# A fourth set of expert weights, and the ranked experts' first load moved behind a gather

## Chip, cores and metric

The kernel runs on one core of a Trainium2 chip. The metric is device time in microseconds (us), the median of three runs. The host only pads x to 3328 rows, pads and transposes the adjacency matrix, and cuts the padding off the result.

## What is computed

One layer of a graph network with 3327 tokens of 256 features, then a mixture of 16 experts of which every token uses two:

```python
# graph attention: x = x + LN(softmax-weighted mean over neighbours of h), h = layernorm(x) @ W, 4 heads of 64
x = x + gnn(layernorm(x), adj, W, a, gamma, beta)
# experts, on xn = layernorm(x)
logits = xn @ gate_w + gate_b                 # (3327, 16)
top_probs, top_idx = top_k(softmax(logits), 2)
dispatch = one_hot(top_idx) * top_probs / sum(top_probs)
hidden = silu(xn @ w1[e]) * (xn @ w2[e])      # w1, w2: 16 x 256 x 512
x = x + sum_e dispatch[:, e] * (hidden @ w3[e])   # w3: 16 x 512 x 256
```

All products are in float32. One expert's three matrices are 0.5 MB each, 1.5 MB together.

## The kernel before

**Two phases.** The graph phase works on 26 tiles of 128 rows in 7 groups. TensorE (PE) multiplies each 0/1 adjacency tile with the rows of h, which are split into a high and a low part (lines 584 and 585), and the matrix streams in on the queue of SyncE (SP). After a group's sums, `finish` normalises the rows, stores them to the DRAM tensor `normed` together with their two experts and weights, and adds the row numbers to per-expert lists. The expert phase walks 19 lists of rows. Lists 0 to 2 are the rows of experts 0 to 2 among the first five groups; they start while the last two groups are being finished. Lists 3 to 5 are the rows of the same three experts from the last two groups (at most 128 rows each). These are what the change's title calls the last groups' first lists. Lists 6 to 18 are the other 13 experts, ranked by how many rows they have, with room for 512 rows down to 336.

**One list** (`take_list`). GpSimd (POOL) gathers the rows of `normed` by an indirect DMA for each 128 rows (line 956) into one of three buffers `xe`; VectorE (DVE) picks each row's weight out of what was gathered (`weigh`, lines 962 and 964, the work `wd`); PE turns the rows (line 1027, result copied by ScalarE, ACT, line 1034); PE multiplies with w1 and w2 in four pieces (line 971), ACT applies silu (line 1044), DVE multiplies (`hid`, line 1047); PE multiplies with w3 (lines 978 and 982); DVE or ACT scales (`y`); POOL adds the rows to the output by an indirect DMA (line 985).

**Weights.** Expert 0's weights go to borrowed buffers. All others are loaded by SP with three DMAs (lines 326 to 328) into a ring of sets of three tiles, `("w", i)`. There are 3 sets: experts 1 and 2 take two of them early and keep them until lists 4 and 5 are done; list 6's expert takes the third. In what follows "w6" is the load for list 6, "w7" the one for list 7, and so on. Which expert list 6 has is known on the chip only: `all_lists` ranks the experts (`names`, line 893 on), and DVE copies the expert numbers into the integer table `table[:, 0]` (line 896), from which SP reads a register (`value_load`, line 1161) before the three DMAs.

**Who sets the order.** Each engine's instructions are written in an order that a planner works out at build time. Every piece of work has an engine, an assumed cost, a rank, works it comes after, and buffers it uses; 80 greedy orders with small random offsets on the works of `finish` are tried, and the one with the shortest replay is written. The works named in `after` only shape this order. On the chip an instruction waits for what its data need: SP's `value_load` waits for the DVE copy into `table`, and a weight DMA waits for the last reader of the set it overwrites. `load_more` (line 941) reads a flag into a register on all engines; a loop for lists that outgrow their room stands at the end and is not entered here.

Of the kernel before, what the change touches and what calls it, by code (L numbers as in the profile page):

```python
# [78 lines left out]
EARLY = 3  # L79
# [135 lines left out]
def gnn_moe(ctx: ExitStack, tc: tile.TileContext, x, adj_t, W, a, gamma, beta, gate_w, gate_b, w1, w2, w3, out):  # L215
    nc = tc.nc
# [64 lines left out]
    expert = const.tile([P, NL], F32, name="expert")  # L281
# [3 lines left out]
    table = const.tile([P, 2, NL], I32, name="table")  # L285
# [54 lines left out]
    gnn, ffn = ExitStack(), ExitStack()  # L340
# [5 lines left out]
    PE, DVE, ACT, POOL, SP = "PE", "DVE", "ACT", "POOL", "SP"  # L346
    T, POOLS = {}, {}
# [18 lines left out]
    def few_h(key):  # L366
# [1 line left out]
                "rs": tiny.tile([P, 2, GT], F32, name="rs", bufs=SLOTS["few_h"])}  # L368

    SLOTS = {"pa": 4, "pt": 2, "ph": 2, "stage": 3, "mask": 3, "pay": 2, "xt": 2, "xnt": 2, "agg": 2, "hp": 2, "hc": 2,  # L370
             "few": 3, "few_h": 3, "xe": 3, "hid": 2, "gate": 3, "y": 6, "w": 3, "weight": 4}
    MAKE = {
        "pa": lambda key: ps_agg.tile([P, CAP], F32, name="pa"),
        "pt": lambda key: ps_tr.tile([P, CAP], F32, name="pt"),
# [23 lines left out]
    plan = Plan(SLOTS, take)  # L398

    def once(key, make):  # L400

        if key not in T:
            T[key] = make()
        return T[key]

    def psum(key):
        return T[key]
# [429 lines left out]
    def numbers(dst, lists, name):  # L837

        empty = tiny.tile(list(lists.shape), F32, name=name, bufs=1)
        nc.vector.tensor_scalar(empty, lists, 0.0, NONE, op0=ALU.is_equal, op1=ALU.mult)  # L840
        nc.vector.scalar_tensor_tensor(dst, lists, -1.0, empty, op0=ALU.add, op1=ALU.add)
# [26 lines left out]
    def all_lists(counted, lists):  # L868
        key = ("ph", "all")

        def make(name, shape):
            return once(("all", name), lambda: tiny.tile([P] + shape, F32, name=name, bufs=1))

        def across(ap):
            return ap[:, None, :].to_broadcast([P, NR, NR])

        def along(ap):
            return ap[:, :, None].to_broadcast([P, NR, NR])

        def ranks():  # L880

            pl = psum(key)
            tokens_of = make("tokens_of", [NE])
            key_, rank, by = make("key", [NR]), make("rank", [NR]), make("by", [NR, NR])
            nc.vector.tensor_copy(tokens_of, pl[:, :NE])
            nc.vector.scalar_tensor_tensor(key_, tokens_of[:, EARLY:], float(NE), number[:, EARLY:], op0=ALU.mult,
                                           op1=ALU.subtract)
            nc.vector.tensor_tensor(by, across(key_), along(key_), op=ALU.is_gt)
            nc.vector.tensor_reduce(rank, by, AX.X, ALU.add)

        def names():
            rank, hotr, by = make("rank", [NR]), make("hotr", [NR, NR]), make("by", [NR, NR])
            nc.vector.tensor_tensor(hotr, across(rank), along(number[:, :NR]), op=ALU.is_equal)
            nc.vector.tensor_tensor(by, hotr, across(number[:, EARLY:]), op=ALU.mult)
            nc.vector.tensor_reduce(expert[:, 2 * EARLY:], by, AX.X, ALU.add)
            nc.vector.tensor_copy(table[:, 0], expert)

        def order():
            return T["hp", "all"].rearrange("p t d -> p (t d)")[:, :NR * CT * NR].rearrange("p (r t e) -> p r t e", r=NR, t=CT)

        def numbered():
            numbers(make("numbered", [NR, CT]), listed[:, EARLY:NE, :], "empty2")

        def sorted_():
            nc.vector.tensor_tensor(order(), make("numbered", [NR, CT]).rearrange("p e t -> p t e")[:, None, :, :].to_broadcast(
                [P, NR, CT, NR]), make("hotr", [NR, NR])[:, :, None, :].to_broadcast([P, NR, CT, NR]), op=ALU.mult)

        def by_ranks():
            nc.vector.tensor_reduce(make("by_rank", [NR, CT]), order(), AX.X, ALU.add)

        def ranked():
            by_rank = make("by_rank", [NR, CT])
            nc.vector.tensor_copy(index[2], by_rank)
            in_out(out_index[2], by_rank, "behind2")

        def rest():

            hotr, by, tokens_of = make("hotr", [NR, NR]), make("by", [NR, NR]), make("tokens_of", [NE])
            full, some = make("full", [NL]), make("some", [1])
            nc.vector.tensor_copy(count[:, EARLY:2 * EARLY], tokens_of[:, :EARLY])  # L920
            nc.vector.tensor_tensor(by, hotr, across(tokens_of[:, EARLY:]), op=ALU.mult)
            nc.vector.tensor_reduce(count[:, 2 * EARLY:], by, AX.X, ALU.add)
            nc.vector.tensor_scalar(behind[:, 2 * EARLY:], expert[:, 2 * EARLY:], float(LIST), None, op0=ALU.mult)
            nc.vector.tensor_scalar(end, behind, float(LIST), None, op0=ALU.add)
            nc.vector.tensor_add(behind, behind, room)
            nc.vector.tensor_tensor(full, count, room, op=ALU.is_gt)
            nc.vector.tensor_copy(table[:, 1], full)
            nc.vector.tensor_reduce(some, full, AX.X, ALU.max)
            nc.vector.tensor_copy(more, some)

        i = plan.add(DVE, 0.7, (1,), [lists], lambda: indices(1))
        w = plan.add(PE, 0.15, (0,), [counted], lambda: tokens_so_far(key), [key])

        r = plan.add(DVE, 1.1, (3, NG, 0), [w], ranks, [key])
        r = plan.add(DVE, 1.2, (3, NG, 0), [r], names)
        o = plan.add(DVE, 0.55, (3, NG, 1), [lists], numbered)
        for cost, piece_ in ((1.4, sorted_), (0.9, by_ranks), (0.6, ranked)):
            o = plan.add(DVE, cost, (3, NG, 1), [r, o], piece_, [("hp", "all")])

        def load_more():  # L940
            many["value"] = nc.values_load(more[0:1, 0:1], min_val=0, max_val=1)

        plan.add(SP, 0.5, (5,), [plan.add(DVE, 2.2, (4,), [o], rest)], load_more)
        return i, r, o
# [52 lines left out]
    GOT = {}  # L997

    def take_list(i, indexed, stored, weights, opened, order):
# [21 lines left out]
            weigh(T["weight", i], XE[i % 3], len(tiles), expert[:, i:i + 1])  # L1021

        wd = plan.add(DVE, 0.4, (2, i, 9), got, weighed, [xek, ("weight", i)])

        def turned(k):
            for t, _ in tiles:
# [4 lines left out]
        for k in range(KC):  # L1031
            key = ("pt", "list", i, k)
            w = plan.add(PE, 0.13 * len(tiles), rank + (0,), got, lambda k=k: turned(k), [key, xek])
# [18 lines left out]
        for t, mm in tiles:  # L1052
            key, yk = ("ph", "list", i, t), ("y", i, t)
            w = plan.add(PE, 8 * 0.217 / PARTS[mm] + 0.1 * (PARTS[mm] > 1), rank + (9 + t,), hids, lambda t=t, mm=mm, key=key: down_products(
                psum(key), w_of(2), hid(), t, mm), [key, hk] + ([wk] if weights else []))
# [4 lines left out]
            def scale(t=t, mm=mm, key=key, yk=yk, helped=helped):  # L1060
# [9 lines left out]
            w = plan.add(ACT if helped else DVE, 0.48 * PARTS[mm], (2, i), [w, wd], scale, [key, yk, ("weight", i)])  # L1070
            ends.append(plan.add(POOL, 1.87, (1, i), [w] + order, lambda t=t, mm=mm, yk=yk: add_rows(
                T[yk], index_of(i, out_index), t, mm, others, i < EARLY), [yk], landing=2.5))
        return ends

# [18 lines left out]
    for made, c0, c1, c in ((landed, H, H + D, 1.0), (summed, 0, H, 0.5)):  # L1095
        means, subtract = center(w_sb, ("ph", "w", c0), c0, c1)
        w = plan.add(PE, c, (0,), [made], means, [("ph", "w", c0)])
# [11 lines left out]
    w = plan.add(PE, 0.8, (2,), [rest], means, [("ph", "gw")])  # L1109
# [7 lines left out]
    for g in range(NG):  # L1117
# [7 lines left out]
        if g == EARLY_GROUP:  # L1125
            i, c = early_lists(c, l)
            tables = [c]
            ready.update({k: (i, list(stored)) for k in range(EARLY)})
        if g == NG - 1:
            i, ranked, o = all_lists(c, l)  # L1130
# [3 lines left out]

    def switch_pools():
        gnn.close()
        POOLS["wmore"] = ffn.enter_context(tc.tile_pool(name="wmore", bufs=3))
        POOLS["hidden"] = ffn.enter_context(tc.tile_pool(name="hidden", bufs=2))
        POOLS["gates"] = ffn.enter_context(tc.tile_pool(name="gates", bufs=3))

# [6 lines left out]
    def more_weights(key, source):  # L1147
        WE[key] = T["w", key]
        load_weights(WE[key], source())

    opened = plan.add(PE, 0.0, (9,), every, switch_pools)
# [3 lines left out]
    def late_weights(i):  # L1155

        if i < EARLY:
            return plan.add(SP, 1.2, (1, 990 + i), [opened] + GOT[i - 1], lambda: more_weights(i, lambda: i), [("w", i)],
                            landing=2.0, size=size)
        return plan.add(SP, 1.6, (1, 1000 + i), [opened, ranked] + GOT[i - 1], lambda: more_weights(  # L1160
            i, lambda: nc.sync.value_load(table[0:1, 0, i:i + 1], min_val=EARLY, max_val=NE - 1)), [("w", i)],
            landing=2.0, size=size)

    order = []
    for i in range(NL):
        of = i if i >= 2 * EARLY else i % EARLY
        if of not in weights:
# [2 lines left out]
        order = take_list(i, indexed, rows + spare[i if i < 2 else 5 if i == 2 else 0], of, [opened, weights[of]], order)  # L1170
# [4 lines left out]
    with tc.If(many["value"] > 0):  # L1175
        with tc.For_i(0, NL) as i:
            e = nc.values_load(table[0:1, 0, bass.ds(i, 1)], min_val=0, max_val=NE - 1)
            full = nc.values_load(table[0:1, 1, bass.ds(i, 1)], min_val=0, max_val=1)
            w = weight_tiles()
            load_weights(w, e)  # L1180
            with tc.For_i(0, full * (NT // AGAIN)) as c:
# [4 lines left out]
                weight = small.tile([P, AGAIN], F32, name="weight_again")  # L1186
# [12 lines left out]
                hid = POOLS["hidden"].tile([P, JC, CAP], F32, name="hid")  # L1199
# [9 lines left out]
                y = POOLS["gates"].tile([P, CAP], F32, name="s").rearrange("p (t d) -> p t d", d=D)  # L1209
# [37 lines left out]
```

## Time and profile before

| | |
|---|---|
| median of 3 runs | 532.24 us (531.89 to 532.77) |
| the profiled execution | 532.32 us, its span 530.6 us, clock 0.997 |
| PE busy | 517.0 us of the span (97%) |
| DVE, ACT, POOL busy | 274.1, 160.8, 213.3 us |
| weight loads on SP's queue | 15 x 3 DMAs of 512 KB, and expert 0's |
| gathers (L956) and row additions (L985) | 61 each, 1051 ns and 1538 ns on POOL |

Times in the views are microseconds from the start of the span. A line of the timeline gives start, length, engine, source line, operation, output and inputs, shape and how many instructions are merged; in square brackets stands the engine's idle time before it and what ended it. PEld is the loading of weights into PE's array. q0 is the DMA queue of the gathers and row additions, q1 that of SP's DMAs. In the waits view the columns are total us, times, and the longest.

### The profile page before, as it was taken

What the parts mean: (1) busy time and instruction counts of PE and PEld (TensorE: products, weight loads), DVE (VectorE), ACT (ScalarE), POOL (GpSimd) and SP (SyncE); (2) the same over time, 40 slices, a digit from 0 to 9 for tenths busy, and PEclk for the clock granted to TensorE, in tenths of its full rate; (3) what the DMA queues carried; (4) which work ended last, traced back from release to release, by engine and by line L of the source; (5) the groups of instructions that cost most, each with busy time, mean ns of one, the idle gap of its engine ahead of it and who ended that gap; (6) DMA issues with size and microseconds to landing.
All of it is one profiled execution on the core that took longest, in us unless ns stands there. A gap on an engine that the chain in (4) does not pass through costs nothing. (4 is left out here: it accounts for less than half of the span.)

```text
span 530.6 us, 8626 instructions
## 1 busy us (share of the span) xinstructions
PE 517.0 (97%) x3005; PEld 406.5 (77%) x3006; DVE 274.1 (52%) x848; ACT 160.8 (30%) x464; POOL 213.3 (40%) x240
## 2 busy tenths in 40 slices
PE   8999999999999999999898999999999999999995
PEld 5889999999999999777686557566566656666674
DVE  6968554967779799689721222212233233323221
ACT  3461145545362650564222201111111111112110
POOL 4320031311030413566677364373475446522333
PEclk9999999999999999999999999999999999999998
DMA  8934879897879893754648564463465546543222
GB/s 277 361 118 126 287 245 316 257 315 258 255 227 369 261 370 118 220 151 105 182 76 274 136 126 120 96 160 112 101 157 143 141 99 156 141 117 70 30 29 28
DMA packets 63394, 94.63 MB, mean 178 GB/s; under 512 B 4846, under 2 KB 36850, under 8 KB 63348
## 3 DMA queue, kind: packets, MB, share of 16 engines
q1 hardware_dynamic: 52308, 80.04, 46.3%
q0 software_dynamic: 10768, 13.75, 15.3%
q8 instruction: 24, 0.39, 0.3%
q10 hardware_dynamic: 272, 0.26, 0.2%
q14 instruction: 22, 0.18, 0.1%
HBM read 81.55 MB, written 13.90 MB: 180 GB/s over the span
## 5 line engine op out<-in xcount | busy, mean ns | idle before, releaser
L584 PE MATMUL pa<-hi,mk 128*128 128x258 f32 x676 | 167.6, 289 | 1.0 <-DVE mk L561 1.0
L585 PE MATMUL pa<-lo,mk 128*128 128x256 f32 x676 | 163.3, 281 | 0.0
L584 PEld LDWEIGHTS pa<-hi,mk 128*128 128x128 f32 x676 | 127.8, 189 | 2.3 <-DVE mk L561 1.2
L585 PEld LDWEIGHTS pa<-lo,mk 128*128 128x128 f32 x676 | 127.5, 189 | 0.1
L985 POOL DMA_INDIRECT out<-y,out_index x61 | 93.8, 1538 | 59.0 <-DVE y L1065 39.9
L971 PE MATMUL pa<-xt,w1e 128*128 128x400 f32 (+8 forms) x272 | 98.9, 486 | 1.7 <-issue 1.7
L1047 DVE TENSOR_TENSOR hid<-s,pa 128x400 f32<-128x400 f32 (+9 forms) x76 | 40.2, 529 | 116.1 <-PE pa L971 91.8
L956 POOL DMA_INDIRECT x<-normed,index x61 | 64.1, 1051 | 86.5 <-PE pt L1027 64.7
L971 PE MATMUL pa<-xt,w2e 128*128 128x400 f32 (+8 forms) x272 | 98.2, 484 | 0.3
L1044 ACT ACTIVATE s<-pa 128x400 f32<-128x400 f32 (+9 forms) x76 | 35.8, 471 | 199.8 <-PE pa L971 191.5
L982 PE MATMUL ph<-w3e,hid 128*128 128x256 f32 (+2 forms) x400 | 89.5, 380 | 0.0
L982 PEld LDWEIGHTS ph<-w3e,hid 128*128 128x128 f32 (+2 forms) x400 | 73.7, 188 | 10.5 <-issue 0.2
L971 PEld LDWEIGHTS pa<-xt,w2e 128*128 128x128 f32 x272 | 49.5, 190 | 37.6 <-issue 18.7
L971 PEld LDWEIGHTS pa<-xt,w1e 128*128 128x128 f32 x272 | 49.2, 190 | 37.8 <-issue 21.9
L561 DVE TENSOR_SCALAR mk<-sg 128x2048 fp32r<-128x2048 f32 (+2 forms) x49 | 54.2, 1106 | 29.9 <-PE pa L585 28.4
L1065 DVE TENSOR_SCALAR y<-ph,weight 128x256 f32<-128x256 f32 (+5 forms) x54 | 26.0, 482 | 72.2 <-PE ph L982 41.0
L650 POOL TENSOR_TENSOR hp<-csum,c 128x512 f32<-128x512 f32 (+1 forms) x14 | 15.1, 1096 | 65.0 <-DVE c L646 65.0
L478 PE MATMUL ph<-w_sb,xnt 128*128 128x260 f32 x104 | 27.2, 397 | 0.4 <-DVE lo L484 0.3
L1034 ACT COPY xt<-pt 128x512 f32<-128x512 f32 (+2 forms) x38 | 17.4, 505 | 20.1 <-PE pt L1027 18.7
L478 PEld LDWEIGHTS ph<-w_sb,xnt 128*128 128x128 f32 x104 | 17.8, 189 | 4.8 <-issue 1.2
L421 POOL TENSOR_SCALAR rs_x<-spread_x 128x4 f32<-128x4 f32 (+1 forms) x7 | 1.8, 259 | 47.3 <-ACT pay L427 44.1
L1027 PEld LDWEIGHTS pt<-ident,x 128*128 128x128 f32 x122 | 14.3, 141 | 7.1 <-issue 6.1
(181 smaller groups left out, 471.4 us busy)
## 6 DMA issues: line engine op xcount, KB each, us to landing
sg<-in_adj_t SPq DMA_DIRECT2D x25, 1024.0 KB
sg<-in_adj_t SPq DMA_DIRECT2D x20, 768.0 KB
w1e<-in_ffn_w SPq DMA_DIRECT2D x15, 512.0 KB
w2e<-in_ffn_w SPq DMA_DIRECT2D x15, 512.0 KB
w3e<-in_ffn_w SPq DMA_DIRECT2D x15, 512.0 KB
normed<-pay SPq DMA_DIRECT2D x5, 520.0 KB
out<-x SPq DMA_DIRECT2D x5, 512.0 KB
sg<-in_adj_t SPq DMA_DIRECT2D x4, 576.0 KB
```

Source lines behind the costliest of these rows:

```text
L478: nc.tensor.matmul(ph[:, :H + D], T["xnt", g, t][:, k, :], w_sb[:, k, :], start=(k == 0), stop=(k == KC - 1))
L561: nc.vector.tensor_scalar(T[mk][:, :m, :n * P], T[sk][:, :m, :n * P], 0.0, None, op0=ALU.is_gt)
L584: nc.tensor.matmul(pa[:, :D + 2], lhs, HI[mg][:, i, H:], start=first, stop=False)
L585: nc.tensor.matmul(pa[:, :D], lhs, LO[mg][:, i, H:], start=False, stop=left[g, t] == 0)
L956: nc.gpsimd.indirect_dma_start(out=xe[:, t, :], out_offset=None, in_=normed[:limit], in_offset=at_rows(idx, t), bounds_check=limit - 1, oo ...
L971: nc.tensor.matmul(p[:, :n], wt[:, k, j * P:(j + 1) * P], xt[:, k, :n], start=(k == 0), stop=(k == KC - 1))
L982: nc.tensor.matmul(py[:m, :D], hid[:, j, t * P:t * P + m], w3e[:, j, :], start=(j == 0), stop=(j == JC - 1))
L985: i = nc.gpsimd.indirect_dma_start(out=out, out_offset=at_rows(idx, t, m), in_=y[:m], in_offset=None, bounds_check=NP - 1, oob_is_err=Fals ...
L1034: xts.append(plan.add(ACT, 0.1 + 0.9e-3 * m, (1, i), [w], lambda k=k, key=key: nc.scalar.copy(xt()[:, k, :m], psum(key)[:, :m]), [key, xtk]))
L1044: nc.scalar.activation(T["gate", i, j][:, :n], psum(key)[:, :n], AF.Silu)
L1047: nc.vector.tensor_mul(hid()[:, j, :n], T["gate", i, j][:, :n], psum(key)[:, :n])
L1065: nc.vector.tensor_scalar(T[yk][:mm], psum(key)[:mm, :D], weight, None, op0=ALU.mult)
```

## The change

The ring of weight sets has 4 sets instead of 3. The copy of the expert numbers into `table` leaves `names` and becomes a DVE work of its own, `tell`, that is planned after the weights of list 4's rows have been picked (`wd` of list 4, which waits for list 4's gather). The ranked experts' loads come after `tell` instead of after `ranked` (the ranking). In the plan w6 no longer comes after list 5's gather, and the load for a later list comes after the gather two lists before it instead of the one before it.

```diff
     SLOTS = {...
-             "few": 3, "few_h": 3, "xe": 3, "hid": 2, "gate": 3, "y": 6, "w": 3, "weight": 4}
+             "few": 3, "few_h": 3, "xe": 3, "hid": 2, "gate": 3, "y": 6, "w": 4, "weight": 4}
...
             nc.vector.tensor_reduce(expert[:, 2 * EARLY:], by, AX.X, ALU.add)
-            nc.vector.tensor_copy(table[:, 0], expert)
...
         wd = plan.add(DVE, 0.4, (2, i, 9), got, weighed, [xek, ("weight", i)])
+        if i == 2 * EARLY - 2:
+
+            told.append(plan.add(DVE, 0.2, (2, i, 9), [wd, ranked], tell))
...
+    def tell():
+        nc.vector.tensor_copy(table[:, 0], expert)
...
-        POOLS["wmore"] = ffn.enter_context(tc.tile_pool(name="wmore", bufs=3))
+        POOLS["wmore"] = ffn.enter_context(tc.tile_pool(name="wmore", bufs=4))
...
-        return plan.add(SP, 1.6, (1, 1000 + i), [opened, ranked] + GOT[i - 1], lambda: more_weights(
+        return plan.add(SP, 1.6, (1, 1000 + i), [opened] + told + (GOT[i - 2] if i > 2 * EARLY else []), lambda: more_weights(
             i, lambda: nc.sync.value_load(table[0:1, 0, i:i + 1], min_val=EARLY, max_val=NE - 1)), [("w", i)],
             landing=2.0, size=size)
...
-    order = []
+    order, told = [], []
```

`EARLY` is 3, so `2 * EARLY - 2` is list 4 and `i > 2 * EARLY` means list 7 on.

## Prediction

> **What bounds the kernel now.** I read the page first: PE is busy 517.0 of 530.6 us, so at most 13.6 us can be won without making PE's work smaller, and the change removes no PE instruction. The waits of PE come next, because they say whether a weight load or a gather ever stops it.
>
> ```profile
> engine line waited for: us in total, times, longest us
> PE pt L1027 <- DMA x<-normed,index: 2.0, 1, 2.0
> PE pa L971 <- issue: 1.7, 2, 1.0
> ...
> PE pa L584 <- DVE mk L561: 1.0, 1, 1.0
> PE pt L708 <- DVE x L692: 1.0, 2, 0.6
> ```
>
> No line says that PE waited for a weight set. Its longest wait is for a gather: 2.0 us, once. Then the windows, cut where PE's work changes, show where the idle time lies.
>
> ```profile
> 0.00:215.81 215.81, 213.00 (x1718) 201.65 (x1720) 161.61 (x524) 92.60 (x302) 51.34 (x110) 1.00 0.78 257
> 215.81:260.32 44.51, 43.52 (x234) 31.28 (x233) 37.73 (x154) 22.11 (x64) 27.29 (x27) 1.00 0.62 175
> 260.32:262.83 2.51, 0.51 (x4) 0.31 (x3) 1.23 (x7) 0.43 (x2) 1.55 (x2) 1.00 0.61 205
> 262.83:288.10 25.27, 23.32 (x160) 20.59 (x160) 6.46 (x23) 6.67 (x21) 19.49 (x17) 1.00 0.59 145
> 288.10:524.71 236.61, 236.61 (x895) 152.70 (x893) 66.61 (x141) 39.01 (x75) 111.35 (x86) 1.00 0.48 114
> ```
>
> First number after the stretch: its length; second: PE busy. From 288.10 (list 6's first product, the first ranked expert) to PE's end PE never idles, so the time is set by when PE gets there. Idle before that: 2.81 us in the graph phase, 0.99 before 260.32, 2.00 at the gather, 1.95 after it. The 1.95 us are no DMA's: they stand at 280.9 to 285.0, and PE's semaphore there rises every 0.73 to 0.77 us per group of four 128-column matmuls that the records space by 0.45 us, so the recorded starts run ahead of PE, and the gap is PE's own arrears. Third, the timelines of PE, POOL and SP around the wait.
>
> ```profile
> 260.32 0.38 PE L1027 MATMUL pt<-ident,x 128*128 128x128 f32 x2
> 262.70 0.30 PE L1027 MATMUL pt<-ident,x 128*128 128x128 f32 x1 [2.00 <-DMA x<-normed,index]
> 262.83 1.06 PE L971 MATMUL pa<-xt,x 128*128 128x128 f32 x8
> ```
>
> ```profile
> 254.42 1.09 POOL L956 DMA_INDIRECT x<-normed,index  x1 [0.98 <-DVE behind L846]
> 255.81 1.82 POOL L956 DMA_INDIRECT x<-normed,index  x1 [0.31 <-issue]
> 257.94 1.00 POOL L956 DMA_INDIRECT x<-normed,index  x1 [0.30 <-issue]
> ```
>
> ```profile
> 254.81 0.40 SPq L326 DMA_DIRECT2D w1e<-in_ffn_w  x1
> 255.39 0.39 SPq L327 DMA_DIRECT2D w2e<-in_ffn_w  x1
> 256.48 0.00 SPq L328 DMA_DIRECT2D w3e<-in_ffn_w  x1
> 277.72 0.38 SPq L326 DMA_DIRECT2D w1e<-in_ffn_w  x1
> ```
>
> The three POOL lines are the gathers of lists 3, 4 and 5. w6 is issued at 254.81, before two of them, although the plan puts it after list 5's: on the chip it waits only for the copy into `table`, done at 253.60, and its set is free. Its packets on q1 run from 255.86 to 261.81. List 4's gather, issued at 255.81, lands at 262.56 (the last event on its semaphore), 6.75 us later; PE, done with list 3's two turns, stands until then, and list 3's products stand behind list 4's turn in PE's order. A gather takes 2.27 to 3.06 us from issue to landing, median 2.59, over the 19 gathers that had under 0.1 us of q1 packets per DMA engine while in flight, and 3.67 to 6.75 us, median 4.34, over the 14 with over 2 us. Two gathers at 209.82 and 211.56 took 3.06 and 2.83 us beside a DVE that was busy 0.81 and 1.00 of their issue, so a busy DVE does not make 6.75.
>
> **The change, part by part.**
>
> *`tell`.* The copy takes 0.18 us (176 ns, L896) wherever it stands. It leaves the chain that ends in the lists' indices, so the three gathers may start 0.1 us earlier: nothing, since list 3's is hidden behind list 2's products, which run to 260.3. It comes back after list 4's `wd`. Queued behind it on DVE are list 5's `wd` and list 3's first `hid`, which sat idle 0.65 us for PE before it started at 264.00: 0.18 us fits there. If that cover were gone, it would cost its 0.18.
>
> *w6 moves.* Without w6 beside it list 4's gather lands at 255.81 + 2.59 to 3.06 = 258.4 to 258.9. DVE does list 4's `wd` after list 2's last `hid`, which ends at 261.40, so `table` is written near 262.0. SP then needs a register load (0.28 us) and up to 0.9 us until the first DMA (253.60 to 254.81 before), so w6 starts at 262.5 to 263.2; if `wd` came first on DVE, at 259.5 to 260. List 5's gather has landed by 257.2 + 3.06 = 260.3, so it is free of w6 too. w6 then runs some 6 to 7 us (w6 took 5.95 us on q1, w7 7.10, w8 6.38) and is there by 271; its reader stood at 288.10. Queued behind the longer wait on SP are `load_more` and w7; the normalised rows were stored at 246.94.
>
> *What PE meets next.* List 3's turns end at 260.70. List 4's turn needs one of two PSUM buffers, freed by ACT's copies, which ran 260.63 to 261.06; list 3's products need both copies. So the products that started at 262.83 can start at 261.06 + 0.05 (the hop from ACT to PE at 281.83) = 261.11. Their PSUM is free, and the w3 products behind them need list 2's last `hid` (261.40), while PE reaches them 0.90 us (262.83 to 263.73) later, at 262.0. So PE gains 262.83 - 261.11 = 1.72 us, and 0.3 us of idle time remains. Nothing from 262.83 to 288.10 named in PE's waits is a DMA, and from 288.10 on PE is full, so the 1.72 us reach the end; the 5.92 us behind PE's last matmul (524.71 to 530.63) stay.
>
> *The fourth set.* w7 needed the set of expert 1, free when list 4 was done, and was issued at 277.72 to 280.81; its reader stood at 309.62, 23 us after its last packet at 286.17. In a fourth set it follows w6 at once, and w8 takes w7's old place, w9 w8's. No PE wait names a weight load, so being earlier earns 0. Its cost is where the burst goes: w6 and w7 together fill q1 from about 263 to 276. The gathers of list 6 are issued at 260.98, 262.28, 263.58 and 264.89 and landed by 267.44; PE turns their rows at 276.59, in the new kernel at 274.87. Even with the worst time seen, 264.89 + 6.75 = 271.6: 3.2 us to spare, so 0. Row additions and list 7's gathers are delayed likewise and are needed after 283. Without this cover each microsecond past 274.87 costs one. SBUF grows by 12 KB per partition in the room that the graph phase leaves; nothing reads it before the sums are done.
>
> *The order.* The random offsets are drawn for works of rank 3 alone, so the added work shifts none; the graph phase should be written as before. If another order were chosen, its waits in the graph phase are the unknown: PE idles 0.34 us from 20 to 100 us and none from 100 to 200, so it could win 0.3 us and lose perhaps 1 (a mask wait, 1.0 us, seen once).
>
> Sum: 532.32 (profiled execution) - 1.72 = 530.60. The median of the three runs is 0.08 us below the profiled execution, so 530.5.
>
> [...]
>
> **The rivals.**
>
> *No gain (chance 0.13).* DVE's dense stretch makes the gather late, not w6. For it: the issue took 1.82 us instead of 1.00, and DVE was busy 1.97 of the 2 us from 256. Against: that is 0.8 of the 4.2 us. If all of it were DVE's, the wait stays: 532.2.
>
> *Part (0.12).* The gather still lands late by a mix of both, for example at 261.9: PE resumes at 262.2 and gains 0.6 us, 531.6; or the order costs about 1 us.
>
> *Slower (0.10).* The double burst holds list 6's four gathers. It runs 263 + 5.95 + 7.10 = 276; if gathers could not pass it, the last would land 0.9 us behind, at 277, against 274.87: a PE wait of 2.1 us, and 0.4 us left as net loss; with the POOL instructions stretched to 1.82 us as well (3 x 0.8), 2.8. It decides from a landing after 276.6. Time 532.6 to 535, say 533. Against it: under w7 the gathers of 279.27 and 280.58 landed in 4.5 and 5.6 us, side by side and not one after the other.
>
> *As forecast (0.65).* 530.5, its own range 530.0 to 531.1.
>
> **How the numbers follow.** About 0.2% (1.06 us) is what a measurement of this kernel can tell from no change, so faster means below 531.2. Faster: 0.65 and a third of the partial case, 0.69. Same: no gain, and the rest of the partial case but 0.02, 0.19. Slower: the rival and that 0.02, 0.12. The range 529.9 to 532.4 holds the forecast, the partial case and no gain; it leaves out the slower rival and a gain above 2.3 us.
>
> **What would show it.** Right: PE's waits have no L1027 wait for a gather at all, or one under 0.5 us; `table` is written by DVE after the second L962 of lists 3 to 5; w6's first DMA stands at 260 to 264 and w7's within 2 us of w6's last; list 4's gather lands in 2.6 to 3.1 us; list 6's first L971 with w1e starts near 286.4 and PE's end comes near 523.0. Wrong: the 2.0 us wait still there without q1 packets beside it (DVE's doing); a new L1027 wait near 275 (list 6's gathers behind two loads); or the times moved before 250 us, which would be another order in the graph phase.

## The result, and the profile after

The changed kernel took 532.26 us (median of four runs, 531.28 to 533.29); the kernel before, run beside it, 532.47. The ratio is 0.9998, with a 95% interval of 0.9976 to 1.0019: no difference that can be measured. The forecast was 530.5.

The profiled execution of the changed kernel took 533.29 us, its span is 531.6 us. The first thing forecast did happen: the gather comes in time. These are POOL's issues of the gathers of lists 3, 4 and 5 and SP's first issue of w6 and of w7, from the two timelines (the same columns as before; an issue's line has no landing, so the landings are taken from the last event on each gather's semaphore):

```profile
254.94 1.10 POOL L955 DMA_INDIRECT x<-normed,index  x1 [0.77 <-DVE behind L846]
256.34 1.81 POOL L955 DMA_INDIRECT x<-normed,index  x1 [0.31 <-issue]
258.45 1.00 POOL L955 DMA_INDIRECT x<-normed,index  x1 [0.30 <-DVE by_rank L908]
```

```profile
263.77 0.38 SPq L326 DMA_DIRECT2D w1e<-in_ffn_w  x1
...
266.08 0.37 SPq L326 DMA_DIRECT2D w1e<-in_ffn_w  x1
```

w6 now starts at 263.77 and no q1 packet runs beside the three gathers. List 4's lands at 259.94, 3.59 us after its issue instead of 6.75. The lines of PE's waits that lie in the expert phase now read:

```profile
PE pa L970 <- ACT s L1046: 1.5, 1, 1.5
...
PE ph L981 <- issue: 0.4, 1, 0.4
...
PE pa L970 <- DVE hid L1049: 0.3, 1, 0.3
PE pt L1029 <- ACT xt L1036: 0.2, 1, 0.2
```

The 2.0 us for the gather are gone. (Line numbers have moved: L970 are the first products, L1029 the turns, L1046 silu, L1049 `hid`, L961 the weigh.) But a wait of 1.5 us for a silu is new. The windows, cut at the starts of list 2, list 3, list 6 and at PE's end, show where the gain stops; the columns are length, then busy time of PE, PEld, DVE, ACT and POOL, then the granted clock, the DMA share and GB/s:

```profile
251.69:261.84 10.15, 9.90 (x43) 7.08 (x42) 9.11 (x35) 2.65 (x7) 6.21 (x6) 1.00 0.33 55
261.84:288.62 26.78, 24.63 (x160) 21.80 (x160) 7.04 (x26) 5.77 (x19) 19.92 (x17) 0.94 0.84 254
288.62:525.64 237.02, 236.88 (x895) 152.56 (x893) 66.74 (x141) 40.12 (x77) 112.55 (x87) 1.00 0.46 107
```

From list 2's first product to list 3's it takes 10.15 us; before it took 262.83 - 250.95 = 11.88. So 1.73 us were won, where 1.72 was forecast. From list 3's first product to list 6's it takes 26.78 us instead of 25.27: 1.51 us were lost again. The rest of the 0.97 us by which this one execution is longer lies elsewhere: 0.74 us before list 2 (whose order is unchanged; the end of the sums lies between 215.6 and 217.2 us in the fourteen profiles), 0.41 us from list 6 to PE's end.

The 0.94 in the second line is part of it. TensorE's granted clock stood at half for 3.41 us of this execution, from 271.81 to 275.22, and that is 1.7 us of work. The loss lies in list 3: from its first product to list 4's first it takes 14.14 us instead of 10.19. From there to list 6 it takes 12.64 instead of 15.08, so that 2.44 of the 3.95 us come back: lists 4 and 5 are less late than they were before. PE's timeline and two lines of DVE's show the stretch; below them stands the first of the two DVE lines in the kernel before:

```profile
261.68 0.33 PE L1029 MATMUL pt<-ident,x 128*128 128x128 f32 x1 [0.25 <-ACT xt L1036]
261.84 1.06 PE L970 MATMUL pa<-xt,x 128*128 128x128 f32 x8
262.74 3.62 PE L981 MATMUL ph<-w3e,hid 128*128 128x256 f32 x16
266.29 1.08 PE L977 MATMUL ph<-w3e,hid 128*64 128x256 f32 x8
267.30 2.05 PE L970 MATMUL pa<-xt,x 128*128 128x128 f32 x16
270.88 0.71 PE L970 MATMUL pa<-xt,x 128*128 128x128 f32 x4 [1.53 <-ACT s L1046]
```

```profile
270.50 0.48 DVE L1067 TENSOR_SCALAR y<-ph,weight 64x256 f32<-64x256 f32 x1 [6.88 <-PE pa L970]
...
272.53 0.23 DVE L961 SCALAR_TENSOR_TENSOR hit<-x,expert 128x8 f32<-128x8 f32 x1 [0.53 <-DMA x<-normed,index]
```

```profile
268.96 0.48 DVE L1065 TENSOR_SCALAR y<-ph,weight 64x256 f32<-64x256 f32 x1 [4.67 <-PE ph L978]
```

L977 at 266.29 is list 2's third product with w3. Its result reaches DVE (`y`, L1067) at 270.50, 8.65 us after list 3's first product; before it was 6.12 us. The recorded starts of the products run ahead of what PE has finished, and here by some 3 us (this one's recorded end is 267.37), until PE stops. Beside this stretch w6 and w7 are on q1, from 265.1 to 278.9. The line at 272.53 is DVE's weigh of list 6, which waits for list 6's gather; it will matter below.

### The profile page after: what moved, and what is told of

It reads as the page before. It is cut to its first block, busy times and chain, and to the rows that moved or that the text cites. A ratio compares the mean times of both kernels' runs of the same rounds, so it can differ in the third digit from the quotient of the medians.

```text
span 531.6 us, 8626 instructions
## 1 busy us (share of the span) xinstructions
PE 519.7 (98%) x3005; PEld 408.8 (77%) x3006; DVE 274.4 (52%) x848; ACT 161.4 (30%) x464; POOL 213.6 (40%) x240
## 5 line engine op out<-in xcount | busy, mean ns | idle before, releaser
L970 PE MATMUL pa<-xt,w1e 128*128 128x400 f32 (+8 forms) x272 | 98.9, 485 | 0.1
L970 PE MATMUL pa<-xt,w2e 128*128 128x400 f32 (+8 forms) x272 | 98.0, 483 | 0.0
L1049 DVE TENSOR_TENSOR hid<-s,pa 128x400 f32<-128x400 f32 (+9 forms) x76 | 40.2, 530 | 111.3 <-PE pa L970 84.0
L1046 ACT ACTIVATE s<-pa 128x400 f32<-128x400 f32 (+9 forms) x76 | 35.7, 471 | 197.5 <-PE pa L970 188.7
L970 PEld LDWEIGHTS pa<-xt,w2e 128*128 128x128 f32 x272 | 49.5, 190 | 36.9 <-issue 18.0
L970 PEld LDWEIGHTS pa<-xt,w1e 128*128 128x128 f32 x272 | 49.1, 190 | 36.3 <-issue 20.3
L1067 DVE TENSOR_SCALAR y<-ph,weight 128x256 f32<-128x256 f32 (+5 forms) x54 | 26.0, 482 | 76.5 <-PE ph L981 42.7
L664 ACT ACTIVATE agg<-agg,c 128x64 f32<-128x64 f32 x76 | 18.8, 337 | 1.9 <-DVE c L646 1.8
```

The costliest lines, as they stand in the source:

```text
L664: nc.scalar.mul(at, at, some("c")[:, 0, t, h:h + 1])
L970: nc.tensor.matmul(p[:, :n], wt[:, k, j * P:(j + 1) * P], xt[:, k, :n], start=(k == 0), stop=(k == KC - 1))
L1046: nc.scalar.activation(T["gate", i, j][:, :n], psum(key)[:, :n], AF.Silu)
L1049: nc.vector.tensor_mul(hid()[:, j, :n], T["gate", i, j][:, :n], psum(key)[:, :n])
L1067: nc.vector.tensor_scalar(T[yk][:mm], psum(key)[:mm, :D], weight, None, op0=ALU.mult)
```

## Experiments

Two theories are tried here. A: the load that was moved (w6, and with the fourth set w7 right behind it) now runs beside list 2's last and list 3's products, makes their results late, and so takes the gain back. C: the gain is lost in PE's own lateness in lists 4 and 5, whatever is loaded. The expectations of the first comparison start from the half clock: their A says that the gain is real and that the half clock takes it back (A1: the two loads together bring it on; A2: one load or none does), and B, there and in the second comparison, that the gain never reaches the end.

Twelve runs were made in three comparisons, each with the kernel before on the same chip: the first on one chip (X in the table), the second on another (Y), the third on a third (Z). The chip of the first result is not known.

"2 to 3" is the time from list 2's first product to list 3's, "3 to 6" from list 3's to list 6's, "third y" the time from list 3's first product to the first DVE instruction that uses list 2's third result, all from one profiled execution. The executions of one kernel spread by 1.2 to 5.2 us, so a profile shows what one of them did and not what the median is made of. The ratio is to the kernel before on the same chip: 532.48 us (X), 532.75 (Y), 529.68 (Z).

| kernel | chip | us | ratio, 95% interval | 2 to 3 | 3 to 6 | third y |
|---|---|---|---|---|---|---|
| before | | 532.24 | | 11.88 | 25.27 | 6.12 |
| after | | 532.26 | 0.9998 [0.9976, 1.0019] | 10.15 | 26.78 | 8.65 |
| after_again | X | 531.96 | 0.9993 [0.9977, 1.0010] | 10.16 | 26.19 | 8.66 |
| tell_only | X | 532.86 | 1.0007 [0.9986, 1.0027] | 10.16 | 26.65 | 7.88 |
| sets_only | X | 532.14 | 0.9990 [0.9976, 1.0005] | 11.49 | 24.47 | 5.92 |
| late_tell | X | 531.24 | 0.9987 [0.9969, 1.0006] | 10.16 | 25.52 | 6.38 |
| no_burst | Y | 531.69 | 0.9986 [0.9968, 1.0004] | 10.16 | 24.97 | 5.71 |
| turn_later | Y | 532.66 | 0.9997 [0.9979, 1.0015] | 10.00 | 24.67 | 6.56 |
| turn_later4 | Y | 532.78 | 1.0006 [0.9990, 1.0022] | 10.00 | 27.05 | 7.96 |
| late_tell3 | Y | 531.99 | 0.9999 [0.9983, 1.0015] | 10.16 | 25.73 | 5.68 |
| before_early | Z | 529.99 | 1.0009 [0.9998, 1.0019] | 11.43 | 22.20 | 5.57 |
| fetch_early | Z | 531.85 | 1.0039 [1.0026, 1.0052] | 10.16 | 26.08 | 5.57 |
| fetch_late | Z | 533.01 | 1.0069 [1.0045, 1.0093] | 10.16 | 25.48 | 5.57 |
| late_tell_again | Z | 531.89 | 1.0034 [1.0021, 1.0048] | 10.16 | 26.70 | 5.57 |

### First comparison: the parts one by one

**after_again** is the changed kernel unaltered.

> The changed kernel again. In its first profile list 4's gather landed in 3.59 us instead of 6.75 and PE's 2.00 us wait was down to 0.25, but TensorE's clock stood at half for 3.41 us (271.81 to 275.22), which is 1.7 us of work, and PE came to list 6 no earlier. Theory A (the gain is real and a clock drop takes it back): executions fall into two kinds, a mean clock of about 0.998 with a span near 529.5 and one of 0.993 to 0.995 with a span near 531, most of them the latter; median ratio 0.998 to 1.000. Theory B (the gain never reaches PE's end, the drop is chance): one kind of execution, ratio 0.999 to 1.001, and clocks as often high as low.

It took 531.96 us and repeats the profile: the same 10.16 us, the same 1.5 us wait for the silu, the third result at 8.66. In this execution the trace's clock record shows TensorE at half its clock for 3.41 us, from 271.7 to 275.1, just behind the gap in PE; that costs 1.7 us of work. Five of its twelve executions have a mean granted clock of 0.995 or less, as such a stretch would give; their median is 532.37, that of the others 531.66. So the half clock goes with some 0.7 us in five executions of twelve, and without it the forecast of 530.5 is still missed by more than 1 us. The gap ahead of the half clock was 1.5 us long; what brings it on isn't shown.

**tell_only** has three sets and the moved copy:

```diff
-            nc.vector.tensor_copy(table[:, 0], expert)
...
+            told.append(plan.add(DVE, 0.2, (2, i, 9), [wd, ranked], tell))
...
+        return plan.add(SP, 1.6, (1, 1000 + i), [opened] + told + (GOT[i - 2] if i > 2 * EARLY else []), lambda: more_weights(
```

> The copy into the table moved behind list 4's weights, but three sets as before, so that w6 comes late and w7 stays where it was (near 278). Theory A1 (the double burst of w6 and w7 beside lists 2 and 3 starves PE and brings the clock drop): no wait for list 4's gather, no drop, 1.5 us less than before, 530.7, clock 0.997. Theory A2 (one burst beside those products is enough, or none): no wait for the gather, but the drop as in the changed kernel, 532.2. If the fourth set were needed for the gain, the wait would be back.

532.86 us. The gather wait is gone, and the late result is there with w6 alone (264.6 to 272.2): third result at 7.88, a PE wait for the silu of 1.4 us. So the fourth set isn't needed for the loss. Nor is the half clock: there is none between lists 3 and 6 in this profile, and from list 3's first product to list 4's first it takes 11.90 us, 1.71 more than before, which is what was won. Neither A1 nor A2 expected this.

**sets_only** has four sets, and the copy where it was:

```diff
-             "few": 3, "few_h": 3, "xe": 3, "hid": 2, "gate": 3, "y": 6, "w": 3, "weight": 4}
+             "few": 3, "few_h": 3, "xe": 3, "hid": 2, "gate": 3, "y": 6, "w": 4, "weight": 4}
...
-        POOLS["wmore"] = ffn.enter_context(tc.tile_pool(name="wmore", bufs=3))
+        POOLS["wmore"] = ffn.enter_context(tc.tile_pool(name="wmore", bufs=4))
```

> A fourth set, the copy into the table where it was. w6 is issued near 254.8 as before and w7 right behind it, both beside the gathers of lists 3 to 6. If w6 makes list 4's gather late: the 2.0 us wait stays or grows (2 to 4 us, 532.3 to 534), and list 6's gathers land up to 4 us later without costing anything. If the fourth set itself paid, 531 or less.

532.14 us. PE's waits still name list 4's gather:

```profile
PE pt L1027 <- DMA x<-normed,index: 1.6, 1, 1.6
```

w7 runs from 265.0 to 270.9, beside the same products as w6 in tell_only, but the third result comes at 5.92. So a load beside these products doesn't always make them late: theory A in its plain form has a miss here.

**late_tell** is the changed kernel with `tell` planned behind list 3's last `hid`, so that w6 and w7 run from 273.2 on, with w8 and w9 behind them until 296.4:

```diff
-            told.append(plan.add(DVE, 0.2, (2, i, 9), [wd, ranked], tell))
+            told.append(plan.add(DVE, 0.2, (2, i, 9), [wd, ranked, HIDS[i - 1][-1]], tell))
```

> Four sets, and the copy planned behind list 3's last hid (about 271) instead of list 4's weights, so that neither gathers of list 3 to 6 nor list 2's and 3's products have a weight load beside them; w6 and w7 run from 272 to 285. Theory A1: no wait for the gather, no stall of PE between 267 and 271, no clock drop, 530.5; with the same burst now beside lists 4 and 5 their products may lag instead. Theory A2: drop as in the changed kernel, 532. If w6 came too late: a wait at list 6's first product (286), 533 or more.

531.24 us, the lowest on this chip, with an interval that includes no difference. The gather wait is gone, the third result comes at 6.38, the wait for the silu is 0.5 us.

### Second comparison: no load at all, and the turns moved instead

**no_burst** leaves out the loads for lists 6 and 7 (these two lists use the weights of experts 1 and 2), and `tell` stands behind list 6's first `hid`, so that no weights are loaded from list 3 to list 6:

```diff
-        of = i if i >= 2 * EARLY else i % EARLY
+        of = i if i >= 2 * EARLY + 2 else 1 + i % 2 if i >= 2 * EARLY else i % EARLY
```

> Leaves out the weight loads for lists 6 and 7 (they use experts 1 and 2), and the copy into the table comes behind list 6's first hid, so that no weight load runs from 255 to about 291. A bound, not a candidate. In the runs so far list 2's three down products were scaled 2.8, 4.55 and 6.1 to 6.4 us after list 3's first product where no load ran beside them, and 3.45, 5.7 and 7.9 to 8.65 where w6 did. Theory A (a weight load beside the products of lists 2 to 5 makes PE finish late): here 2.8, 4.55, 6.1, no wait of PE in lists 3 to 5 over 0.3 us, list 3's first product to list 6's first product 23 to 24 us (before 25.3, changed 26.2 to 26.8), no clock drop. Theory C (PE's lateness lies in the 128-column products themselves): lists 4 and 5 late as before, 25 us.

531.69 us. List 2's results are on time (5.71). But list 5's silus still come every 1.5 us, with no load beside them. From ACT's timeline of this kernel:

```profile
280.41 0.28 ACT L1044 ACTIVATE s<-pa 128x128 f32<-128x128 f32 x1 [1.60 <-PE pa L970]
281.90 0.28 ACT L1044 ACTIVATE s<-pa 128x128 f32<-128x128 f32 x1 [1.21 <-PE pa L970]
```

So lists 4 and 5 have a lateness that isn't a weight load's (theory C), and list 2's third result has one that was seen only with a load beside it (A). Even with no load from list 3 to list 6 the time isn't clear of the kernel before: 0.9986 [0.9968, 1.0004].

**turn_later** and **turn_later4** leave `tell` out. The kernel before, with three and with four sets, has the turns of lists 4 and 5 planned behind list 2's w3 products, so that list 4's late gather holds up nothing:

```diff
-            w = plan.add(PE, 0.13 * len(tiles), rank + (0,), got, lambda k=k: turned(k), [key, xek])
+            w = plan.add(PE, 0.13 * len(tiles), rank + (0,), got + (DOWN[2] if i in (4, 5) else []), lambda k=k: turned(k), [key, xek])
```

> The kernel before, w6 where it was (254.8, beside list 2's wide products and the gathers), but PE's turns of lists 4 and 5 are planned behind list 2's down products, so that nothing on PE needs the late gathers before 267. Theory A: the 2.0 us wait gone with list 4's gather still landing 6 to 7 us after its issue, no load beside lists 2 and 3's products, so no lateness there: 1.0 to 1.7 us less, 530.8 to 531.5. Theory B (PE's wait costs nothing at the end): 532.4. The turns of later lists stand together in this order; if that hurts, it shows as waits at line 1027 or 971 behind 288.

> The same with four sets: w7 follows w6 at about 263 instead of 278. Theory A: w7 beside list 2's down products and list 3 may cost there what it no longer costs beside list 5: between 530.5 and 532. If double loads as such were harmless, 530.5.

turn_later took 532.66 us and has no gather wait: the 1.9 us from list 2 to list 3 are won with w6 where it was. Theory A expected 530.8 to 531.5 for it; the median is nearer to B's 532.4. Its profile is of an execution of 531.25 us, where all took 530.49 to 535.11, and no trace shows where the longer ones lose the gain; from list 6 to PE's end this order takes 0.44 us more. turn_later4 took 532.78; its w7 runs from 263.5 to 270.6, and the late result (7.96) and the silu wait (1.4 us) are back. sets_only, which lacked the lateness, has w7 at nearly the same times; but there it starts 1.2 us after list 3's first product and here 2.5. Whether that decides wasn't tried.

**late_tell3** is late_tell with three sets.

> The late copy (behind list 3's last hid) with three sets, so only w6 runs at 272 to 279 and w7 follows list 4. Against the late copy with four sets (532.48 to 531.24 in the last comparison) it tells what the fourth set does: theory A says little, 531.0 to 531.8, no low clocks; if the fourth set carried that gain, 532.4.

531.99 us, third result 5.68: again no lateness without the load beside it. The time lies between the two that were expected, so what the fourth set does for late_tell stays open.

### Third comparison: PE's own instructions, and another chip

q8 brings instructions in blocks of 16 KB: 24 of them in the kernel before, one per some 250 of PE's 6011 recorded instructions (196 to 295 from one block to the next), so they are read here as PE's program. In three of the four kernels with the late third result PE issued nothing while such a block was on its way: in the changed kernel the fetch ran from 269.79 to 270.73, and 4065 PE instructions had been recorded at its start and at its end; after_again and tell_only show the same (4065, 4062). In turn_later4, and in the kernels without the lateness, the fetch came at 266.6 to 267.5 (sets_only: 270.64), and 11 to 19 instructions were issued meanwhile. Whether PE stands still for its program when such a block is fetched beside a weight load was the question (theory F, against theory S: the load slows the products themselves). It was tried by moving the fetches: more, smaller warm-up products at the start of PE's program.

```diff
-        for _ in range(6):
+        for _ in range(4):      # fetch_early, before_early; 3 in fetch_late
             nc.tensor.matmul(psum(("pt", "warm")), ones, ones[:, None, :].to_broadcast([P, CAP // P, P]), start=True, stop=True)
+        for _ in range(20):     # 45 in fetch_late
+            nc.tensor.matmul(psum(("pt", "warm"))[:8, :8], ones[:, :8], ones[:, :8], start=True, stop=True)
```

**fetch_early** is the changed kernel with 36 more PE instructions in front, **fetch_late** with 84, **before_early** the kernel before with 36, **late_tell_again** the same kernel as late_tell.

> The changed kernel, but two of the six warm-up products at the very start of PE's program are replaced by 20 small ones (8 columns), so that PE has 36 more instructions in front of everything else, and the place where its program is read on (16 KB on q8, once per about 250 PE instructions) moves some 36 instructions earlier among the expert phase's work: wanted near 263 us, before w6's burst (265.1), where the changed kernel wanted it near 267 and got it at 269.79, with no PE instruction issued meanwhile (4065 records before and after the fetch). Theory F (the stall behind list 2's down products is PE waiting for its own instructions, which wait behind the weight load): the fetch lies before 265, list 2's three results come at about 2.8, 4.6 and 6 us after list 3's first product instead of 3.47, 5.70 and 8.65, the 1.5 us wait for list 3's silu goes to 0.5 or less, from list 3's first product to list 6's is 25.3 us or less instead of 26.2 to 26.8, and the time is 530.5 to 531.3. Theory S (the burst slows the products themselves, at SBUF or elsewhere): 26.2 or more again, the wait again, and 531.9 to 532.3.

> The changed kernel with three of the six warm-up products and 45 small ones: 84 more PE instructions in front. The program is then wanted near 259 us, free of any load, and again near 283 to 284 us, where w8's and w9's burst (280.6 to 295.8) has begun. Theory F: nothing late behind list 2's down products, but a new gap of 1 to 2 us in PE, with no PE instruction issued while the fetch is out, at about 284.5 to 287, in list 5's products; from list 3's first product to list 6's 26 us or more, time near 532. Theory S: the lateness behind list 2's down products as in the changed kernel (third result 8 us or more after list 3's first product), none added near 285.

> The kernel before with the same 36 more PE instructions in front as fetch_early has. Its own fetch in this place lay at 267.53, between two weight loads, so both theories expect no change from the shift: the wait for list 4's gather again at about 1.5 to 2 us, 25.0 to 25.6 us from list 3's first product to list 6's, and the same time as the kernel before to within 0.3 us. If it is faster by 1 us or more, the shift itself brings something elsewhere, and fetch_early's time has to be read against this one.

> late_tell once more, beside the kernels that move PE's instruction fetch. Both theories expect what it had: no gather wait, the fetch near 266.6 ahead of the load (273 on), about 25.5 us from list 3's first product to list 6's, and 531.2 to 531.6. If it is within 0.3 us of the kernel before here, its 1.2 us in the first comparison were chance.

The chip answered another question. Here the kernel before takes 529.68 us, 2.8 and 3.1 us less than on the other two. before_early equals it, and its profile shows where the difference is: its windows from list 3 to list 6 and after it, and two of list 5's silus, below which stand the same two silus of the first profile of the kernel before.

```profile
263.18:285.38 22.20, 22.20 (x160) 20.36 (x160) 6.47 (x23) 6.90 (x21) 17.00 (x15) 1.00 0.63 161
285.38:522.00 236.62, 236.62 (x895) 152.63 (x893) 66.83 (x141) 39.00 (x75) 114.30 (x88) 1.00 0.49 114
```

```profile
280.75 0.28 ACT L1044 ACTIVATE s<-pa 128x128 f32<-128x128 f32 x1 [0.62 <-PE pa L971]
281.64 0.28 ACT L1044 ACTIVATE s<-pa 128x128 f32<-128x128 f32 x1 [0.62 <-PE pa L971]
```

```profile
283.78 0.28 ACT L1044 ACTIVATE s<-pa 128x128 f32<-128x128 f32 x1 [1.95 <-PE pa L971]
285.29 0.28 ACT L1044 ACTIVATE s<-pa 128x128 f32<-128x128 f32 x1 [1.23 <-PE pa L971]
```

0.89 us from silu to silu instead of 1.51, and 22.20 us from list 3 to list 6 instead of 25.27. All four profiles of this chip have the quick steps in list 5, none of the eight from X and Y has them throughout. From list 6 on the chips agree (236.62 and 236.61 us). So the lateness in lists 4 and 5 doesn't come from the 128-column products alone; it goes with the chip, or with the hour. Why isn't known.

On this chip, where PE isn't late, the moved load does cost time, at a place that neither theory had. In fetch_early, from the timelines of DVE and PE:

```profile
273.29 0.23 DVE L961 SCALAR_TENSOR_TENSOR hit<-x,expert 128x8 f32<-128x8 f32 x1 [3.31 <-DMA x<-normed,index]
...
273.63 0.29 DVE L1049 TENSOR_TENSOR hid<-s,pa 128x128 f32<-128x128 f32 x1
```

```profile
273.98 0.70 PE L981 MATMUL ph<-first_w,hid 128*128 128x256 f32 x2 [1.98 <-DVE hid L1049]
```

L961 is the weigh of list 6's rows. DVE stands 3.31 us for list 6's gathers: the last two were issued at 264.65 and 265.95, beside w6 and w7, and landed at 272.64 and 273.17, 8.00 and 7.22 us later. List 3's last `hid` is queued behind the weigh, and PE's last w3 products of list 3 wait 1.98 us for it. fetch_late has the same (2.66 us on DVE, 1.33 on PE), and then a second one (its profile is of one of the three executions at 531.3 to 531.8 us; the other three took 534.2 to 535.2, at clocks of 0.991 to 0.995):

```profile
285.71 0.33 PE L1029 MATMUL pt<-ident,x 128*128 128x128 f32 x1 [1.46 <-DMA x<-normed,index]
```

That is list 7's turn; its fourth gather, issued at 279.88 beside the next pair of loads, landed at 285.66. late_tell_again took 531.89 us, where 531.2 to 531.6 was expected. Its load comes later, and it has no wait for list 6's gathers, but the longest one for list 7's:

```profile
285.16 0.48 PE L1029 MATMUL pt<-ident,x 128*128 128x128 f32 x1 [2.71 <-DMA x<-normed,index]
```

In fetch_early and late_tell_again a stretch of 3.41 us at half clock comes with the wait (from 275.3 and from 285.0), 1.7 us more.

fetch_early differs from the changed kernel, and before_early from the kernel before, by the same 36 instructions. So on this chip the change is worth 531.85 - 529.99 = +1.86 us, 0.35% slower, though the gather wait that it removes is 1.5 us here too. In the two profiles: 1.27 us won from list 2 to list 3, 3.88 us lost from list 3 to list 6, of which 1.98 are the wait for `hid` and 1.7 the half clock. The half clock isn't needed for the loss: the other four executions of fetch_early, at clocks of 0.997 to 0.999, took 531.28 to 531.89 us. The wait less the gain would make 0.7 us there; no trace shows what makes up the rest, some 1.1 us.

Theory F isn't settled by this. Its forecast for the third result came true (5.57 instead of 8.65), those for the time (530.5 to 531.3) and for list 3 to list 6 (25.3 or less) did not, and late_tell_again and before_early have 5.57 as well, so the chip may explain it. The gap that F expected in fetch_late isn't there: a fetch at 281.58 lay in the middle of a load, and 19 PE instructions were issued while it ran. A run of the changed kernel itself on this chip, and of fetch_early on one of the others, would tell; neither was made. Theory S in its plain form fails on this chip: w6 and w7 run beside list 2's last products from 265.0 on in fetch_early and from 265.2 in fetch_late, and these aren't late.

No version here beats the kernel before clear of the noise: late_tell had the lowest time on chip X, 0.9987 [0.9969, 1.0006], and is slower on Z, 1.0034 [1.0021, 1.0048]. What the last comparison points to, list 6's weigh planned behind list 3's last `hid` and w6 left where it was, wasn't tried.

## Why the prediction was right and wrong

**Right: why the gather was late.** With w6 away list 4's gather takes 3.59 us (3.5 to 3.7 in all kernels that moved the load), with it 6.75 (5.9 to 6.8 in the five profiles that have it there). This is the test between w6 and DVE that the "No gain" rival asked for, and w6 has 3.2 of the 4.2 us. The remaining 1.0 over a clean gather's 2.59 goes with POOL's issue of 1.81 us instead of 1.00, which is unchanged; the forecast of 2.6 to 3.1 us left that out, at no cost, since the rows are needed only at about 261.

**Right: the gain at the spot.** 1.73 us against 1.72. `tell` ran at 262.73 in 0.17 us, behind the second of the small weighs. w6 started at 263.77, in the interval of 260 to 264, and w7 0.8 us behind w6's last issue. The order of the graph phase didn't change.

**Wrong: "so the 1.72 us reach the end".** The step rested on two readings. The first: nothing in PE's waits from 262.83 to 288.10 is a DMA, so nothing there would change. That is a reading of the old profile, in which the load didn't stand there. In the changed kernel, and in after_again and tell_only on chip X, the load that was moved in came with a silu wait of 1.4 to 1.5 us (not in late_tell), and list 6 started about where it had. List 3 to list 6 cost 0.9 to 1.5 us more than in the first profile of the kernel before, against 1.7 won. That a load there makes the results late isn't shown: sets_only, fetch_early and fetch_late have one and no lateness.

**Wrong: "3.2 us to spare, so 0".** The forecast of list 6's landing was good: 271.6 as the worst, 272.41 measured. What failed is when it is needed. The prediction took PE's turn, at 276.59 before and so at 274.87 with 1.72 us won. The first reader is DVE's weigh of list 6, with list 3's last `hid` queued behind it. In the first profile of the kernel before:

```profile
270.66 0.22 DVE L962 SCALAR_TENSOR_TENSOR hit<-x,expert 128x8 f32<-128x8 f32 x1
270.91 0.16 DVE L964 TENSOR_REDUCE weight<-hit 128x4 f32<-128x8 f32 x1
271.34 0.29 DVE L1047 TENSOR_TENSOR hid<-s,pa 128x128 f32<-128x128 f32 x1 [0.27 <-ACT s L1044]
```

With the same 1.72 us won, the weigh is due at 268.94, and by that the cover was -2.7 us and not 3.2. In the changed kernel's profile PE was itself late and DVE's wait was 0.53 us; on chip Z it was 3.31 (fetch_early) and 2.66 (fetch_late). Likewise for list 7, whose landing the prediction didn't work out ("needed after 283"): PE wanted its last gather at 282.45 in late_tell_again and at 284.25 in fetch_late, and it landed at 285.12 and 285.66. The "Slower" rival had the mechanism, the double burst against list 6's gathers, but looked for it in PE's turns alone and asked for a landing after 276.6. A landing after about 269 was enough.

**Half right: "PE's own arrears".** The lateness of lists 4 and 5, with which the 1.95 us of idle at 280.9 to 285.0 goes, is there without any weight load (no_burst), so no weight load makes it; gathers and row additions still run there. But it isn't PE's in general: chip Z doesn't have it, and its cause stays open. Where PE is late a late gather is met late too; that this is why the change costs nothing on chip X and 0.35% on Z is argued, not shown.

**The range** held the time by luck. The forecast was 530.5; 532.26 was inside because the "No gain" rival's 532.2 was in the range, and that rival's reason, a gather that stays late, is not what happened. The gather came in time, and the gain was lost behind it.

## What to carry to other kernels

When a transfer is moved away from a wait, cost the place where it goes like the place that it leaves: list every transfer that will then be in flight beside it, and for each the first instruction on any engine that reads what it brings, with what is queued behind that reader. A small step on a side engine, here a weigh of 0.23 us that DVE runs ahead of a `hid` that PE needs, can be the first reader, 6 us ahead of the one on the main engine. And a gain of 0.3% is smaller than the difference between two chips (0.5% here), so compare on more than one before it is believed.

## What the runs showed of the hardware that was not expected

- The same kernel took 532.48, 532.75 and 529.68 us on three chips. As far as one profile from each side shows (the first of the kernel before, whose chip isn't known, and before_early on Z), the difference lies in some 25 us of small products: 25.27 against 22.20 us, with a granted clock of 1.00 in both.
- A PE gap of 1.5 to 2.7 us came with 3.41 us at half clock in four profiles (the changed kernel, after_again, fetch_early, late_tell_again), but gaps of 1.3 to 2.0 us also passed without one (before, tell_only, sets_only, turn_later4, before_early, fetch_late).
- Gathers beside a pair of weight loads took up to 8.00 us (fetch_early; 7.91 in after_again), and row additions up to 8.50 (late_tell3; 7.99 in fetch_early), against 2.6 us at the median for a gather with no load beside it.
